# Order of the first six half products of a gated, quantized layer, and the way slot 2's weights are turned

## The chip, the cores and the metric

One core of one Trainium2 chip. The metric is device time of one execution in microseconds (us). A core has TensorE (PE, matrix products into PSUM banks), VectorE (DVE), ScalarE (ACT), GpSimd (POOL) and SyncE (SP), whose queue issues nearly all DMA transfers here. Each engine works through its own instructions strictly in the order in which the program lists them; engines wait for one another by semaphores.

## The reference

```python
# x: (4, 1024, 512), cond: (4, 128), norm_w: (512, 128), up_w: (4096, 512), down_w: (512, 2048)
scale = cond @ norm_w.T + 1.0
ms = jnp.mean(x * x, axis=-1, keepdims=True)
h = x * (scale[:, None, :] * jax.lax.rsqrt(ms + EPS))
u = h @ up_w.T
val, gate = jnp.split(u, 2, axis=-1)
h = val * jax.nn.gelu(gate, approximate=False)
hq = h + stop_gradient(act_quant(h) - h)              # 8 bit, one scale a token
wq = down_w + stop_gradient(weight_quant(down_w) - down_w)   # three values, one scale
y = hq @ wq.T
return y + x
```

## The kernel before

**Slots, halves, batches.** The 2048 hidden columns are cut into 16 slots of 128 (`NJ`); a slot needs 128 rows of the value weights and 128 of the gate weights of `up_w`. The 1024 tokens of a batch are cut into two halves of 512. "Half (j,h)" is slot j for half h of the first batch's tokens: a product for the gate (`pg`), Gelu on ScalarE, a product for the value (`pv`), then one VectorE instruction that scales and multiplies (L643, the "gate step"). `plain_half` (L635) does this; `plain_first` (L645) is half (0,0) with the work that brings in the data woven between its products. Each product is twelve matmuls of 128x128 by 128x512, because weights and tokens are each split into a high and a low half-precision part.

The first batch is computed by plain products. Batches 1 to 3 use a scheme with seven smaller products (L594, L668), for which seven combinations of each slot's weights are made once in the first batch, written to DRAM (`s_dram`) and loaded again for every batch.

**From a weight row to a product.** `w_load` (L284) loads a slot's weights by rows; `w_range` (L317) finds a power of two for each row (a reduction and three small instructions on VectorE); `w_gain` multiplies it with the token factor; `w_scale` (L328) scales the rows, on GpSimd for slots below `ROWS` and on ScalarE for the others. The weights must then be turned so that the contracted index lies on the partitions, in one of two ways:

- slots below `ROWS` (0, 1, 2): `w_turn` (L337), eight TensorE transposes into two PSUM banks; `w_high` (ScalarE) and `w_low` (VectorE) split the banks into high and low parts; `w_evac` (L381) copies the turned weights to `wf(j)` for the sums.
- the other slots: `w_rows` (L352) splits the rows (ScalarE copies, L357, VectorE subtracts, L358), then one turned DMA transfer on SP's queue (L359) of 512 KB.

`s_sums` (L385, GpSimd, four instructions, L391 to L394) forms the combinations in the buffer `sf`; `s_all` splits them (`s_high` on ScalarE, L403; `s_low` on GpSimd, L407) and writes them to DRAM (`s_spill`). For slots below `ROWS` the combinations are made of turned weights, so `s_load_x` and `s_load_y` (L431, L435) load them plainly (L429); for the others they are kept as rows and the load turns them (L427).

**Places.** `H` has 18 slots of buffer, which hold hidden results and, early on, other data. `X0 = H[:, 4:8]` holds the eight token tiles of the first batch (128 tokens each, tile n in half a slot). `W_SLOT`, `W_EARLY` and `ROW_SLOT` say which slot of `H` holds a slot's weight rows and their split.

**The start.** SP's queue first loads norm weights, token tiles 0 to 3, slot 0, slot 1, token tiles 4 to 7, slot 2 (L987 to L993). `first_sum` forms a tile's sum of squares (one instruction, 128x512, ScalarE or VectorE), `rsqrt` one small VectorE step and a power on GpSimd (L505), `first_scale` scales a tile, `first_turn` turns it by four TensorE transposes (L969), `first_high` and `first_low` split it (ScalarE L973, VectorE L977). `other_half` does the last three for tiles 4 to 7. `w_turn` of slots 1 and 2 takes place inside half (0,0) and half (1,0); `other_half` inside half (2,0).

The order of the halves is (0,0), (1,0), (2,0), (0,1), (1,1), (2,1), then (3,0), (3,1), (4,0) and so on. Between (2,0) and (0,1) VectorE's list has `cond_scale_rest` (L190) and `cond_largest`: the scale factors of batches 1 to 3 and their largest values, `mx`. `cond_over` (L209) turns `mx` on TensorE (`pm`), ahead of half (1,1). All of this is an order written out by hand (`manual_schedule`).

Of the kernel before, what the change touches and what calls it, by code (L numbers as in the profile page):

```python
# [51 lines left out]
def glu_quant_kernel(  # L52
# [17 lines left out]
    NK = D // P  # L70
# [103 lines left out]
    def cond_load_rest():  # L174
        v = cond[1:].rearrange("b c -> (b c)").partition_broadcast(P)
        ACT.dma_start(out=cb[:, 1:].rearrange("p b c -> p (b c)"), in_=v)
# [90 lines left out]
    sg0 = sm.tile([P, NJ, 2], F32, name="sg_0", tag="sg")  # L267
    up_v = up_w.rearrange("(t j p) d -> j p t d", t=2, p=P)
    W_SLOT = {1: 12, 2: 13, 0: 14}
    W_EARLY = {6: 9, 7: 10, 8: 11}  # L270
    ROW_SLOT = {3: 8, 4: 15, 5: 16}
    iv = {}
    pw = {}

    def wn(j):
        return H[:, W_EARLY.get(j, W_SLOT[j % 3])]

    def wf(j):

        return H[:, 11 if j == 2 else 15 + j % 2].rearrange("p t (n f) -> p (t n) f", n=2)  # L280

    sf = H[:, 17].rearrange("p t (n f) -> p (t n) f", n=2)

    def w_load(j, ts=(1, 0)):  # L284
        if j > 2:
            SP.dma_start(out=wn(j), in_=up_v[j])
            return
        for t in ts:
            SP.dma_start(out=wn(j)[:, t], in_=up_v[j][:, t])
# [27 lines left out]
    def w_range(j, t0=0, t1=2):  # L317
        w_factor(j, w_largest(j, t0, t1), t0, t1)

    def w_gain(j):  # L320
        DVE.tensor_tensor(sg0[:, j, :], sw[:, j, :], dx[:, 0:1].to_broadcast([P, 2]), ALU.mult)

    ROWS = 3
    LATE = 6

    def w_scale(j, ts=(1, 0), eng=None):  # L328
        eng = eng or (ACT if j >= ROWS else POOL)
        for t in ts:  # L330
            w, r = wn(j)[:, t], iv[j][:, t : t + 1]
            if eng is ACT:
                ACT.activation(w, w, AF.Copy, scale=r)
            else:
                eng.tensor_scalar(w, w, r, 1.0, ALU.mult, ALU.mult)

    def w_turn(j, banks=None, ts=(1, 0)):  # L337
        if j not in pw:
            pw[j] = banks or [po_bank(f"pw_{j}_{t}") for t in (1, 0)]
        for t in ts:  # L340
            n = 1 - t
            for k in range(NK):
                PE.transpose(  # L343
                    pw[j][n][:, k * P : (k + 1) * P], wn(j)[:, t, k * P : (k + 1) * P], ident
                )
# [6 lines left out]
    def w_rows(j):  # L352

        v = H[:, ROW_SLOT.get(j, 15 + j % 2)].bitcast(F16).rearrange("p t d -> p (t d)")
        n = v.rearrange("p (n w f) -> p n w f", n=4, w=2)
        f = wn(j).rearrange("p t (n f) -> p (t n) f", n=2)
        ACT.copy(n[:, :, 0], f)  # L357
        DVE.tensor_tensor(n[:, :, 1], f, n[:, :, 0], ALU.subtract)  # L358
        SP.dma_start_transpose(  # L359
            s_tile(j)[:, 3:7].rearrange("p n w (k f) -> p (n w k) f", k=2), v  # L360
        )

    def w_high(j, ts=(1, 0)):
        gate, a21, a22 = a_parts(j)
        g, v = (p.rearrange("p (n f) -> p n f", n=2) for p in pw[j])
        if 1 in ts:
            ACT.copy(gate[:, :, 0], g)
        if 0 in ts:
            ACT.copy(a21[:, 0], v[:, 0])
            ACT.copy(a22[:, 0], v[:, 1])  # L370

    def w_low(j, ts=(1, 0)):
        gate, a21, a22 = a_parts(j)
        g, v = (p.rearrange("p (n f) -> p n f", n=2) for p in pw[j])
        if 1 in ts:
            DVE.tensor_tensor(gate[:, :, 1], g, gate[:, :, 0], ALU.subtract)
        if 0 in ts:
            DVE.tensor_tensor(a21[:, 1], v[:, 0], a21[:, 0], ALU.subtract)
            DVE.tensor_tensor(a22[:, 1], v[:, 1], a22[:, 0], ALU.subtract)

    def w_evac(j):  # L381
        for n in range(2):
            ACT.copy(wf(j)[:, 2 * n : 2 * n + 2].rearrange("p n f -> p (n f)"), pw[j][n])

    def s_sums(j):  # L385
        if j >= ROWS:
            v = wn(j).rearrange("p t (n f) -> p t n f", n=2)
            a11, a12, a21, a22 = v[:, 1, 0], v[:, 1, 1], v[:, 0, 0], v[:, 0, 1]
        else:
            a11, a12, a21, a22 = (wf(j)[:, n] for n in range(4))  # L390
        POOL.tensor_tensor(sf[:, 0], a21, a22, ALU.add)  # L391
        POOL.tensor_tensor(sf[:, 2], a11, a21, ALU.subtract)
        POOL.tensor_tensor(sf[:, 1], sf[:, 0], a11, ALU.subtract)
        POOL.tensor_tensor(sf[:, 3], a12, sf[:, 1], ALU.subtract)  # L394
# [29 lines left out]
    def s_load(g, c0, c1, turn=False):  # L424
        s, d = s_tile(g)[:, c0:c1], s_dram[g % NJ, :, c0 * 2 * HALF : c1 * 2 * HALF]
        if turn:
            SP.dma_start_transpose(s.rearrange("p c w (k f) -> p (c w k) f", k=2), d)  # L427
        else:
            SP.dma_start(out=s.rearrange("p c w f -> p (c w f)"), in_=d)  # L429

    def s_load_x(g):  # L431
        s_load(g, Y_TO, C_ALL)
        s_load(g, 0, Y_FROM, g % NJ >= ROWS)

    def s_load_y(g):  # L435
        if g % NJ < ROWS:
            s_load(g, Y_FROM, Y_TO)
        else:
            s_load(g, Y_FROM + 1, Y_TO)
            s_load(g, Y_FROM, Y_FROM + 1, True)  # L440


    wmean = cpool.tile([P, 1], F32, name="wmean")
# [59 lines left out]
    def rsqrt(ssq, rs, eng=POOL):  # L503
        eng.tensor_scalar(ssq, ssq, 1.0 / D, EPS, ALU.mult, ALU.add)  # L504
        POOL.tensor_tensor(rs, ssq, neghalf[:, : rs.shape[-1]], ALU.pow)  # L505
# [129 lines left out]
    def plain_half(j, h, between=nothing):  # L635
        pg = bank(*(("A", 2) if h or j == 1 else ("B", 1)), name=f"pg_{j}_{h}")
        plain(j, 1, h, pg)
        t1 = wpool.tile([P, TOK], F32, name=f"g_{j}_{h}", tag="t1")
        ACT.activation(t1, pg, AF.Gelu, scale=gain(j, 1))
        between()  # L640
        pv = bank("E", 2, name=f"pv_{j}_{h}")
        plain(j, 0, h, pv)
        DVE.scalar_tensor_tensor(h_half(j, h), pv, gain(j, 0), t1, ALU.mult, ALU.mult)  # L643
# [279 lines left out]
    def first_load(n, m=1):  # L923
        SP.dma_start(
            out=X0[:, n : n + m],
            in_=xf[n * P : (n + m) * P, :].rearrange("(s p) d -> p s d", p=P),
        )
# [4 lines left out]
    def first_sum(n, eng=ACT):  # L932
        v, j, a = X0[:, n], junk[:, n % 4], ssq0[:, n : n + 1]
        if eng is ACT:
            ACT.activation(j, v, AF.Square, accum_out=a)
        else:
            eng.scalar_tensor_tensor(j, v, 1.0, v, ALU.mult, ALU.mult, accum_out=a)
# [21 lines left out]
    def first_scale(n, eng):  # L959
        r = rs0[:, n : n + 1]  # L960
        if eng is ACT:
            ACT.activation(X0[:, n], X0[:, n], AF.Copy, scale=r)
        else:
            eng.tensor_scalar(X0[:, n], X0[:, n], r, 1.0, ALU.mult, ALU.mult)
# [6 lines left out]
    def first_high(h, k, pt):  # L971
        c = slice(h * TOK, (h + 1) * TOK)
        ACT.activation(XP[:, 0, k, c], pt, AF.Copy, scale=scT[:, k, 0:1])  # L973

    def first_low(h, k, pt, eng=DVE):
        c = slice(h * TOK, (h + 1) * TOK)
        eng.scalar_tensor_tensor(  # L977
            XP[:, 1, k, c], pt, scT[:, k, 0:1], XP[:, 0, k, c], ALU.mult, ALU.subtract
        )
# [7 lines left out]
    first_load(0, 2)  # L987
    first_load(2, 2)
    w_load(0)
    w_load(1)  # L990
    first_load(4, 2)
    first_load(6, 2)
    w_load(2)  # L993
    keep_warm(3)
    pc = cond_first_row()
# [32 lines left out]
    w_range(0, 0, 1)  # L1028
    first_high(0, 0, ptx[0])
    w_high(0, (1,))  # L1030
    w_low(0, (1,))
    w_scale(0, (0,))
    w_gain(0)
    first_high(0, 1, ptx[1])
    first_high(0, 2, ptx[2])
    first_high(0, 3, ptx[3])
    cond_load_rest()
    w_range(1)
    w_gain(1)
# [3 lines left out]
    def second_part():  # L1043
        w_turn(0, ts=(0,))
        w_high(0, (0,))
        w_low(0, (0,))
        w_scale(1, (1,), ACT)
        for k in range(1, NK):
            first_low(0, k, ptx[k])
        ACT.activation(start_t, neghalf[:, 0:1], AF.Gelu)  # L1050


# [92 lines left out]
    def second_slot():  # L1145
        w_turn(1)
        w_high(1)
        w_low(1, (1,))
        w_range(2)
        w_gain(2)  # L1150
        w_scale(2)
        w_low(1, (0,))

    def third_slot():
        w_turn(2)
        w_high(2)
        w_low(2)
        w_evac(2)
        first_scale(4, ACT)
        first_scale(5, DVE)  # L1160
        first_scale(6, ACT)
        first_scale(7, DVE)

    def other_half():
        ptx = [po_bank(f"ptx_1_{k}") for k in range(3)] + [bank("A", 2, name="ptx_1_3")]
# [7 lines left out]
    w_load(3)  # L1173
    for n in range(4, ND):
        d_load(n)
    w_evac(0)
    w_evac(1)
    first_sum(4)
    first_sum(5)
    first_sum(6, DVE)  # L1180
    first_sum(7, DVE)
    rsqrt(ssq0[:, 4:8], rs0[:, 4:8], DVE)
    plain_half(1, 0, third_slot)
    w_load(4)
    s_sums(0)
    w_range(3)
    w_gain(3)
    plain_half(2, 0, other_half)
    w_load(5)
    for n in (2, 3):  # L1190
        d_load(n)
# [2 lines left out]
    s_sums(1)  # L1194
    cond_scale_rest()
    mx = cond_largest(1, B)
    plain_half(0, 1)
    w_range(4)
    w_gain(4)
    w_scale(4)  # L1200
# [3 lines left out]
    for n in D_SUM[0]:  # L1204
        d_sum(n)
    pm = cond_over(mx, 1, B, "po")
    plain_half(1, 1)
    w_load(6)
    for n in (0, 1):
        d_load(n)  # L1210
# [402 lines left out]
```

## Time and profile before

| What | Value |
|---|---|
| Runs | 728.81, 730.6, 730.28 us; median 730.28 |
| The profiled execution | 727.59 us, of it span 725.8 us |
| TensorE products, first 20 us | 17.23 us busy |
| TensorE products, 20 to 40 us | 19.78 us busy |
| TensorE products, 40 to 60 us | 19.69 us busy |
| TensorE products, 60 to 125 us | 65.0 us busy |
| TensorE clock granted | 1.00 throughout |
| Turned weight transfers (L359) | landing 4.3 to 6.7 us after issue, median 4.4 |
| Turned loads of combinations (L427) | 78 of them, issue median 1.39 us, landing 2.7 to 5.1, median 3.7 |
| Plain loads of combinations, 170 to 202 us (L429) | landing 2.7 to 4.2 us, median 3.4 |

A line of the profile names engine, source line, operation, tile, shape and count. In a timeline the first two numbers are start and duration in us; in square brackets stands how long the engine had been idle before, and what ended that. TensorE's matmuls are pipelined, so durations of neighbours overlap and the distances between starts tell what they cost.

### The profile page before, as it was taken

To read this page: it belongs to the slowest core of one execution; us is meant where nothing else is said; L and a number is where in the kernel's file an instruction comes from. 1 tells how busy PE (TensorE), PEld (TensorE's weight loads), DVE (VectorE), ACT (ScalarE), POOL (GpSimd) and SP (SyncE) were. 2 spreads that over 40 slices of the span, in tenths; PEclk is the share of its full clock that TensorE was granted. 3 is DMA by queue.
4 is the path that set the end of the run, shared out by engine and by line. 5 is a ranking of instruction groups with operands and counts; after the bars stand their busy time and mean duration, and the time that the engine had idled before them with its cause. 6 is when DMAs were issued, how large, how long until landed. Compare 5 with 4: busy or idle time off the path is not lost.

```text
span 725.8 us, 10153 instructions
## 1 busy us (share of the span) xinstructions
PE 719.1 (99%) x3664; PEld 359.2 (49%) x3664; DVE 581.7 (80%) x828; ACT 398.2 (55%) x627; POOL 193.5 (27%) x206
## 2 busy tenths in 40 slices
PE   8999999999999999999999999999999999999998
PEld 4544444444444446665444445665444444445844
DVE  8877888985698899787689897687678888755897
ACT  6869876772337674554335676544433665332374
POOL 1479897775100033440000030360020000000100
PEclk9999999999999999999999999999999999999999
DMA  7669998988354654876734646775934455442253
GB/s 265 224 188 299 291 287 237 263 190 227 117 103 102 131 156 129 203 170 164 181 98 101 131 102 179 195 158 162 219 102 102 86 118 101 88 115 89 98 180 116
DMA packets 203982, 117.30 MB, mean 162 GB/s; under 512 B 165382, under 2 KB 174487, under 8 KB 203932
## 3 DMA queue, kind: packets, MB, share of 16 engines
q1 hardware_dynamic: 203642, 116.33, 62.9%
q8 instruction: 28, 0.46, 0.3%
q10 hardware_dynamic: 290, 0.33, 0.1%
q14 instruction: 22, 0.18, 0.1%
HBM read 54.22 MB, written 23.09 MB: 107 GB/s over the span
## 4 chain that ended last, share of the span: by engine, by line
PE 95%; DVE 3%; DMA 1%; ACT 0%; issue 0%; SPq 0%; ACTq 0%
PE A L600 33%; PE E L600 17%; PE pg L615 11%; PE pv L615 10%; PE po L868 8%; PE B L600 8%; PE po_end L820 4%; PE po L820 1%; DMA H<-in_x_dram 1%; DMA SXY<-H 1%; DVE gm L734 1%; PE ptx L969 0%; PE pv L658 0%; DVE R L977 0%; PE pw L343 0%; PE po_B L868 0%
## 5 line engine op out<-in xcount | busy, mean ns | idle before, releaser
L600 PEld LDWEIGHTS <-SXY 128*128 128x128 f16 x2016 | 197.1, 98 | 232.4 <-issue 0.6
L600 PE MATMUL A<-R,SXY 128*128 128x512 f16 x1152 | 266.3, 379 | 0.0
L600 PE MATMUL E<-R,SXY 128*128 128x512 f16 x576 | 140.0, 379 | 0.1
L698 DVE SCALAR_TENSOR_TENSOR H<-A,sg,t 128x512 f32<-128x512 f32 x48 | 36.0, 750 | 69.8 <-PE A L600 69.7
L792 DVE TENSOR_TENSOR H<-H,am 128x1024 f32<-128x1024 f32 x64 | 76.2, 1217 | 0.0
L615 PEld LDWEIGHTS <-SXY 128*128 128x128 f16 x486 | 47.5, 98 | 57.5 <-DMA SXY<-H 0.8
L750 POOL PARTITION_ALL_REDUCE am<-R x8 | 14.3, 1793 | 228.9 <-DVE R L736 228.9
L711 ACT ACTIVATE t<-t,sg 128x512 f32<-128x512 f32 x48 | 34.6, 721 | 66.7 <-DVE t L708 66.5
L600 PE MATMUL B<-R,SXY 128*128 128x512 f16 x288 | 70.0, 379 | 0.0
L734 DVE TENSOR_REDUCE gm<-H 128x512 f32<-128x1024 f32 x56 | 69.0, 1232 | 1.0
L615 PE MATMUL pg<-R,SXY 128*128 128x512 f16 x252 | 57.8, 379 | 0.3 <-DMA SXY<-H 0.3
L615 PE MATMUL pv<-R,SXY 128*128 128x512 f16 x234 | 54.4, 380 | 0.0
L695 ACT ACTIVATE t<-B,sg 128x512 f32<-128x512 f32 x48 | 33.0, 687 | 36.2 <-PE B L600 36.2
L678 ACT COPY t<-A 128x512 f32<-128x512 f32 x48 | 27.9, 582 | 39.8 <-PE A L600 39.5
L504 POOL TENSOR_SCALAR ssq<-ssq 128x2 f32<-128x2 f32 x12 | 3.8, 320 | 172.1 <-ACT xt L534 122.8
L868 PE MATMUL po<-wd,R 128*128 128x256 fp8e4 x384 | 48.5, 273 | 0.0
L800 ACT ACTIVATE H<-H 128x1024 f32<-128x1024 f32 x38 | 39.9, 1050 | 14.3 <-DVE H L792 14.3
L690 ACT COPY v<-E 128x512 f32<-128x512 f32 x48 | 28.1, 585 | 30.8 <-PE E L600 27.5
L868 PEld LDWEIGHTS <-R 128*128 128x128 bf16 (+1 forms) x416 | 40.7, 98 | 8.6
L717 DVE SCALAR_TENSOR_TENSOR H<-v,sg,t 128x512 f32<-128x512 f32 x48 | 37.5, 782 | 7.9 <-ACT t L711 7.9
L736 DVE TENSOR_TENSOR R<-R,gm 128x512 f32<-128x512 f32 x56 | 41.6, 743 | 1.3
L714 DVE TENSOR_TENSOR v<-A,v 128x512 f32<-128x512 f32 x48 | 32.9, 685 | 12.1 <-PE A L600 11.0
(207 smaller groups left out, 982.3 us busy)
## 6 DMA issues: line engine op xcount, KB each, us to landing
SXY<-s_dram SPq DMA_DIRECT2D x57, 256.0 KB, 3.0
s_dram<-SXY SPq DMA_DIRECT2D x18, 384.0 KB, 3.0
H<-in_L_cond_up_w_dram SPq DMA_DIRECT2D x13, 512.0 KB, 5.2
SXY<-s_dram SPq DMA_DIRECT2D x39, 128.0 KB, 3.1
xr<-in_x_dram SPq DMA_DIRECT2D x19, 256.0 KB, 3.1
out_dram<-xr SPq DMA_DIRECT2D x19, 256.0 KB, 2.5
H<-in_x_dram SPq DMA_DIRECT2D x8, 512.0 KB, 8.3
R<-in_L_cond_down_w_dram SPq DMA_DIRECT2D x8, 512.0 KB, 6.1
```

Source lines behind the costliest of these rows:

```text
L600: PE.matmul(o, s[:, w, k, :], tv[:, :, c, l, k, :], start=start and n == 0, stop=stop and n == len(TERMS) - 1, skip_group_check=True,)
L615: PE.matmul(ps, a[k // 2][:, w, k % 2, :], XP[:, l, k, h * TOK : (h + 1) * TOK], start=n == 0, stop=n == len(terms) - 1,)
L695: ACT.activation(cur["t1"], pb, AF.Gelu, scale=gain(g, 1))
L698: DVE.scalar_tensor_tensor(h_half(g - 1, 0), prev["A"], gain(g - 1, 0), prev["t1"], ALU.mult, ALU.mult)
L711: ACT.activation(prev["t2"], prev["t2"], AF.Gelu, scale=gain(g - 1, 1))
L717: DVE.scalar_tensor_tensor(h_half(g - 1, 1), prev["v"], gain(g - 1, 0), prev["t2"], ALU.mult, ALU.mult)
L734: DVE.tensor_reduce(gm[0], v, AX.X, ALU.max, apply_absolute_value=True)
L736: return [largest, lambda: DVE.tensor_tensor(m, m, gm[0], ALU.max)]
L792: DVE.tensor_tensor(v, v, r.to_broadcast([P, 2, TOK]), ALU.mult)
L800: ACT.activation(v, v, AF.Copy, bias=MAGIC)
L820: PE.matmul(po.rearrange("p (y c o) -> p y c o", c=2, o=P), q[:, a, h, j], wd8[:, :, j // n, j % n, :, y0:y1].rearrange("p c o y -> p y c o"),
L868: PE.matmul(po, w[:, j], m, start=start and j == 0, stop=stop and j == n - 1, skip_group_check=True,)
```

## The change

The order of the halves becomes (0,0), (1,0), (0,1), (1,1), (2,0), (2,1). `ROWS` goes from 3 to 2, so slot 2 takes the way of the later slots: scaled by ScalarE, split as rows, turned by a DMA transfer (its rows in `H` slot 16). `w_evac` and `wf` are gone: the combinations of slots 0, 1 and 2 are formed from the rows, too, and all loads of combinations turn them. Slots 3, 4 and 5 get weight places of their own (`H` slots 11, 6, 7; 6 and 7 hold token tiles 4 to 7 until they are turned). Token tiles 4 to 7 are loaded ahead of slot 1; their sums of squares move into half (0,0), `other_half` from half (2,0) into half (1,0), and slot 1's second scaling from ScalarE to GpSimd. `w_range`, `w_gain`, `w_scale` and `w_rows` of slot 2 stand between halves (1,0) and (0,1).

```diff
-    W_EARLY = {6: 9, 7: 10, 8: 11}
-    ROW_SLOT = {3: 8, 4: 15, 5: 16}
+    W_EARLY = {3: 11, 4: 6, 5: 7, 6: 9, 7: 10, 8: 11}
+    ROW_SLOT = {2: 16, 3: 8, 4: 15, 5: 16}
...
-    ROWS = 3
+    ROWS = 2
...
-    def w_evac(j):
-        for n in range(2):
-            ACT.copy(wf(j)[:, 2 * n : 2 * n + 2].rearrange("p n f -> p (n f)"), pw[j][n])
...
     def s_sums(j):
-        if j >= ROWS:
-            v = wn(j).rearrange("p t (n f) -> p t n f", n=2)
-            a11, a12, a21, a22 = v[:, 1, 0], v[:, 1, 1], v[:, 0, 0], v[:, 0, 1]
-        else:
-            a11, a12, a21, a22 = (wf(j)[:, n] for n in range(4))
+        v = wn(j).rearrange("p t (n f) -> p t n f", n=2)
+        a11, a12, a21, a22 = v[:, 1, 0], v[:, 1, 1], v[:, 0, 0], v[:, 0, 1]
...
     def s_load_x(g):
         s_load(g, Y_TO, C_ALL)
-        s_load(g, 0, Y_FROM, g % NJ >= ROWS)
+        s_load(g, 0, Y_FROM, True)
 
     def s_load_y(g):
-        if g % NJ < ROWS:
-            s_load(g, Y_FROM, Y_TO)
-        else:
-            s_load(g, Y_FROM + 1, Y_TO)
-            s_load(g, Y_FROM, Y_FROM + 1, True)
+        s_load(g, Y_FROM + 1, Y_TO)
+        s_load(g, Y_FROM, Y_FROM + 1, True)
...
     w_load(0)
-    w_load(1)
     first_load(4, 2)
     first_load(6, 2)
+    w_load(1)
     w_load(2)
...
     w_high(0, (1,))
+    w_scale(0, (0,))
+    first_sum(4, DVE)
     w_low(0, (1,))
-    w_scale(0, (0,))
     w_gain(0)
     first_high(0, 1, ptx[1])
     first_high(0, 2, ptx[2])
     first_high(0, 3, ptx[3])
+    first_sum(5)
...
         w_high(0, (0,))
         w_low(0, (0,))
-        w_scale(1, (1,), ACT)
-        for k in range(1, NK):
-            first_low(0, k, ptx[k])
+        w_scale(1, (1,))
+        first_sum(6)
+        first_sum(7)
+        first_low(0, 1, ptx[1])
+        first_low(0, 2, ptx[2])
+        rsqrt(ssq0[:, 4:8], rs0[:, 4:8], DVE)
+        first_low(0, 3, ptx[3])
...
     def second_slot():
         w_turn(1)
         w_high(1)
-        w_low(1, (1,))
-        w_range(2)
-        w_gain(2)
-        w_scale(2)
-        w_low(1, (0,))
-
-    def third_slot():
-        w_turn(2)
-        w_high(2)
-        w_low(2)
-        w_evac(2)
         first_scale(4, ACT)
         first_scale(5, DVE)
-        first_scale(6, ACT)
-        first_scale(7, DVE)
+        w_low(1)
...
-    w_evac(0)
-    w_evac(1)
-    first_sum(4)
-    first_sum(5)
-    first_sum(6, DVE)
-    first_sum(7, DVE)
-    rsqrt(ssq0[:, 4:8], rs0[:, 4:8], DVE)
-    plain_half(1, 0, third_slot)
+    first_scale(6, ACT)
+    first_scale(7, DVE)
+    plain_half(1, 0, other_half)
     w_load(4)
     s_sums(0)
+    w_range(2)
+    w_gain(2)
+    w_scale(2)
     w_range(3)
     w_gain(3)
-    plain_half(2, 0, other_half)
+    w_rows(2)
+    plain_half(0, 1)
     w_load(5)
...
     cond_scale_rest()
     mx = cond_largest(1, B)
-    plain_half(0, 1)
+    plain_half(1, 1)
...
     pm = cond_over(mx, 1, B, "po")
-    plain_half(1, 1)
+    plain_half(2, 0)
```

More of the change, by code (lines that the diff above doesn't have):

```diff
@@ L276, in wn @@
         return H[:, W_EARLY.get(j, W_SLOT[j % 3])]
-    def wf(j):
-        return H[:, 11 if j == 2 else 15 + j % 2].rearrange("p t (n f) -> p (t n) f", n=2)
     sf = H[:, 17].rearrange("p t (n f) -> p (t n) f", n=2)
```

## The prediction

> **What bounds the kernel now.** I read the page first: engine totals, then TensorE's share by slice.
>
> ```profile
> span 725.8 us, 10153 instructions
> PE 719.1 (99%) x3664; PEld 359.2 (49%) x3664; DVE 581.7 (80%) x828; ACT 398.2 (55%) x627; POOL 193.5 (27%) x206
> PE   8999999999999999999999999999999999999998
> ```
>
> TensorE is busy for 99% of the span and only the first and last slice fall below 9. Its own pause list (who waited for whom, TensorE alone) shows what it ever waits for (the two lines left out are 0.4 and 0.2 us, ahead of 14 us):
>
> ```profile
> PE pz L985 <- DVE eps L915: 1.5, 1, 1.5
> PE pg L658 <- ACT SXY L367: 0.7, 1, 0.7
> ...
> PE pg L615 <- DMA SXY<-H: 0.3, 1, 0.3
> PE pm L211 <- DVE mx L204: 0.2, 1, 0.2
> ```
>
> All of it lies in the first 50 us. So the change can win only TensorE instructions that it removes plus these few waits, and can lose whatever new wait it puts there. The stretch that matters is from the end of half (0,0) at 19.68 us to the start of the fifth half at 38.34 us; TensorE's timeline there:
>
> ```profile
> 22.27 1.04 PE L343 MATMUL pw<-ident,H 128*128 128x128 f32 x8
> 23.15 0.60 PE L615 MATMUL pv<-R 128*128 128x512 f16 x2
> ...
> 28.33 1.91 PE L969 MATMUL ptx<-ident,H 128*128 128x128 f32 x16
> 30.07 2.75 PE L615 MATMUL pv<-R 128*128 128x512 f16 x12
> ...
> 38.23 0.27 PE L211 MATMUL pm<-ident,mx 128*3 128x128 f32 x1 [0.22 <-DVE mx L204]
> 38.34 2.75 PE L615 MATMUL pg<-R,SXY 128*128 128x512 f16 x12
> ```
>
> Starts are what counts (the ends overlap): twelve products take 2.59 us, a half 5.18; the eight turns of slot 2's weights 23.15 - 22.27 = 0.88; the sixteen turns of the second half's tokens 30.07 - 28.33 = 1.74. Work between 19.68 and 38.34 is 3 x 5.18 + 0.88 + 1.74 = 18.16 of 18.66 us, so about 0.50 us is the `pm` transpose and its wait. The chain of waits says who sets that: VectorE, not TensorE.
>
> ```profile
> 30.67 2.73 DVE R L977 x4
> 33.39 0.66 DVE H L643
> 34.05 1.68 DVE H L197
> ```
>
> **Removed: slot 2's turns on TensorE.** Eight transposes, -0.88 us, with TensorE busy on both sides. The high/low splits and the evacuations of slots 0 to 2 (ScalarE L383, about 0.58 each, six of them) go too; ScalarE and VectorE had idle time there, so they give nothing by themselves.
>
> **Moved: loads and half (0,0).** Slot 1's weights now follow all eight token tiles in SP's queue. Token loads 4-5 and 6-7 are issued at 4.31 and 5.1 us and take 8.3 us, so the last landed at 13.4; slot 1's second half takes that place and byte count, hence also 13.4. Slot 1's range starts at 13.27 now, so it is 0.15 late, and the extra VectorE square sum of tile 4 (0.69) fits the 0.70 us for which VectorE waits at 12.60. From there: reciprocal ready at 15.23 (15.08 now), GpSimd scales both halves of slot 1 by 16.7 (2 x 0.69), before its turns (17.08 now). Slot 0's second low parts end at 16.27 and 16.60; TensorE wants them at 16.22 and 16.65, so it slips about 0.1. The small rsqrt step (0.17 + gap) sits ahead of the last low part of the tokens, which ends near 18.77 against a need of 18.72: another 0.1. I take **+0.20** for half (0,0), between 0 (data earlier) and +1.2, if another 256 KB came ahead of them, 1.0 us at the first slice's 265 GB/s. On ScalarE three square sums (0.63 each) move ahead of the Gelu table load; the first fits the 0.61 idle at 14.92, the other two replace the 0.73 scale that GpSimd takes, so slot 1's high part starts 0.55 later, 18.27, against a need of 19.88.
>
> Half (1,0) then starts at 19.88. Its low weights are needed after four products, 0.87 later, at 20.75. VectorE first scales tile 5, once GpSimd's power (1.06) has ended near 19.1: 0.49 alone (9.77 us), 0.82 beside GpSimd (25.67 us); I take 0.82, because the sums of slot 0 run then. The low part follows, 0.69 (18.35 us), done at about 20.6: no wait, slack 0.1. Were GpSimd idle it would be 0.4. The Trainium skill ("SBUF — State Buffer", Who interferes with whom) says more: a `tensor_scalar` in a two-port mode and GpSimd exclude each other for a whole instruction. Behind one whole sum (0.72) the scale would end at 20.3, the low part at 21.0, and 0.2 to 0.3 us would be added to the sum; the row of 0.82 shows only 0.33 of blocking.
>
> The token turns stay, now inside half (1,0). Tiles 6 and 7 are scaled by 22.7, turned from 22.5 on in order 4 to 7: no wait. So half (1,0) ends at P = 19.88 + 5.18 + 1.74 = 26.80.
>
> **Added: the chain for slot 2 on VectorE.** Slot 3's present chain gives the lengths, from ScalarE's, VectorE's and SP's timelines:
>
> ```profile
> 42.40 1.03 ACT L357 CAST H<-H 128x1024 f16<-128x1024 f32 x1
> ...
> 43.46 1.23 DVE L358 TENSOR_TENSOR H<-H 128x1024 f16<-128x1024 f32 x1 [2.28 <-ACT H L357]
> ...
> 44.76 1.90 SPq L359 DMA_TRANSPOSE SXY<-H  x1
> ```
>
> After P, as after half (2,0) now (next group 32.66, gate 33.31), VectorE is free 0.65 later; gate step 0.66; range of slot 2 up to its reciprocal 1.80 (27.91 to 29.71); ScalarE scales and copies, VectorE subtracts 2.33 after the reciprocal (41.13 to 43.46); range of slot 3 fits in that gap; subtract 1.13 to the next start. So the gate of half (0,1) starts at P + 0.65 + 0.66 + 1.80 + 2.33 + 1.13 = P + 6.57, although its products were done at P + 5.18. Behind it in VectorE's order stand the condition sums (L197 to L204), for which `pm` waits, and behind `pm` on TensorE the whole of half (2,0). From gate to that half takes 38.34 - 33.31 = 5.03: start at P + 11.60 = 38.40. TensorE would be there at P + 10.36. The gap, 1.24, replaces 0.50: **+0.74**.
>
> The transfer itself: issue 3.63 after the reciprocal (41.13 to 44.76), P + 6.74 = 33.54; landing 4.37 later (the chain's `DMA SXY<-H`), 37.91, ahead of 38.40 by 0.49. Rows of that line go from 4.3 to 6.7, the tokens' turned transfers to 7.7. I take 4.37: that row, like this one, has an empty queue ahead. The bounds: 0 and 6.7 + 33.54 - 38.40 = +1.84. The Trainium skill differs with itself here: "Advanced Engine Details and Errata" (X-Bar Transpose (TRN2)) has turned transfers as fast as regular ones, "DMA: Bandwidth & Descriptors" (Latency and other measured facts) 261 GB/s where the middle dimension is not contiguous, an estimated 2.0 us for these 512 KB against 1.3 to 1.5. By either the data would be there before VectorE, and the sum would not move.
>
> SP's queue is in order: the loads of slot 5 and of two parts of the down weights now stand behind this transfer and go out near 35.5 instead of 23. Their readers come after 48 us; 1.5 MB at the first slice's 265 GB/s is 5.7 us. No cost; without that slack they would delay slot 3's transfer at about 45 us.
>
> **After 38.40** the order on all engines equals the present one from 38.34, with half (2,0) in the place of (1,1). VectorE sets both slot 3's transfer and the start, so the 0.31 wait at 49.17 stays. Slot 2's spill in three pieces adds two SP issues of about 0.5 with slot 5's transfer due more than 5 us ahead of its use.
>
> **Moved: loads of slots 0 to 2 in batches 1 to 3.** Nine slots, two turned transfers each instead of plain ones. Issue 1.39 and 1.19 against about 0.5; landing 3.7 (at most 5.1) against 3.4. They go out about one slot of 9.07 us ahead; issue plus landing is at most 6.5 of that. 39 slots already load so, and no TensorE wait falls there. Cost 0; without any lead, the excess of the part needed first, 9 x (0.89 + 0.3) = +10.7.
>
> **Sum:** +0.20 - 0.88 + 0.74 = +0.06. The profiled execution took 727.59 (span 725.8 and 1.8 around it), so 727.65; the median of the runs is 2.69 above it, 730.28 + 0.06, put up to the next tenth: **730.4 us**.
>
> **Rivals.** A difference under 0.3% (2.2 us) can't be told from none here.
> - *The gain is kept.* If the condition sums are ready in time, the transfer decides, 37.91 + 0.05: 0.38 less than now; if it too is early, -0.88 - 0.39 + 0.20 = -1.07. 729.2 to 729.9. For it: all the work is there, only its order is against it. Against: VectorE's order is fixed, and ScalarE's copy stands in between.
> - *Slot 2's weights come late* (the other side). Its packets share the engines with the 1.5 MB issued right behind: a landing 6.7 after issue, the longest row of its line, gives 40.2, 1.8 after VectorE is ready, of which slot 3's 0.31 is won back: 731.9. All 1.5 MB ahead of it, 5.3 us at the 299 GB/s of the fourth slice, gives 43.2 and 734.9. Priced between them, 733.4. It decides from a landing time of 4.9 us on. For: one row of 6.7 in a busy stretch. Against: the 44.76 transfer was also followed by loads, 3 us on.
> - *The turned loads miss their slot*: up to +10.7, 741.1. Against: 39 slots show no wait.
> - *It doesn't do what it says*: TensorE no longer turns slot 2, but stops as long for a number that has nothing to do with slot 2. That is my forecast.
>
> **Chances.** Forecast (729.9 to 731.2) 0.57; gain kept 0.17; late transfer 0.18, half of it past 732.5; missed slots 0.08. Faster by over 0.3% has no mechanism, only scatter of runs (728.81 to 730.6): 0.07. Slower: 0.09 + 0.08 + 0.04 scatter = 0.21. Same 0.72. The range runs from 728.6, below the kept gain, to 733.4, the late transfer's price.
>
> **What would show it.** TensorE's wait for `pm` of about 1 us instead of 0.2 and half (2,0) near 38.4; turned transfer out near 33.5 and landed by 38; no third set of weight turns; half (1,0) starting near 19.9; no TensorE wait after 55 us. A TensorE wait on a transfer into `R` before half (2,0), a first half ending after 20.5, or waits at the batches' starts would make it wrong.

## The result, and the profile after

| Kernel | Median, us | Lowest to highest | Runs |
|---|---|---|---|
| before | 728.75 | 728.12 to 730.82 | 14 |
| after | 730.44 | 729.39 to 732.19 | 14 |

The ratio of after to before is 1.0018, 95% interval 1.001 to 1.0027: 0.7 to 2.0 us slower, under the 2.2 us named in the prediction as what can't be told from no change, but a loss all the same. The forecast of 730.4 us was made from an early median of 730.28 for the kernel before; with more runs that median came down by 1.5 us and the change cost about 1.7, so the two errors cancel: that the time came out so near is luck. The difference, not the time, has to be explained: +0.06 was forecast.

The page of the kernel after (its span, engine totals, TensorE by slice):

```profile
span 729.3 us, 10132 instructions
PE 720.3 (99%) x3656; PEld 359.0 (49%) x3656; DVE 582.6 (80%) x824; ACT 396.4 (54%) x622; POOL 193.2 (26%) x205
PE   8989999999999999999999999999999999999998
```

TensorE has eight instructions less (x3656 against x3664), the turns of slot 2's weights. A new 8 stands in the third slice, 36 to 55 us. TensorE's own waits say what it is (engine, tile, line, what it waited for, total, times, longest):

```profile
PE pg L601 <- DMA SXY<-H: 1.8, 1, 1.8
...
PE pm L211 <- DVE mx L204: 1.0, 1, 1.0
```

Both existed before, at 0.3 and 0.2. TensorE's timeline, in which line 601 is the plain product (615 before):

```profile
7.89 3.77 PE L971 MATMUL pz<-H 128*128 128x512 f16 x9
11.50 1.91 PE L955 MATMUL ptx<-ident,H 128*128 128x128 f32 x16
...
21.58 2.87 PE L601 MATMUL pg<-R,SXY 128*128 128x512 f16 x12
24.29 1.91 PE L955 MATMUL ptx<-ident,H 128*128 128x128 f32 x16
...
40.19 0.27 PE L211 MATMUL pm<-ident,mx 128*3 128x128 f32 x1 [1.04 <-DVE mx L204]
40.52 2.76 PE L601 MATMUL pg<-R 128*128 128x512 f16 x12
...
52.85 2.76 PE L601 MATMUL pg<-R,SXY 128*128 128x512 f16 x12 [1.79 <-DMA SXY<-H]
```

Half (1,0) starts at 21.58, half (2,0) at 40.52, half (3,0) at 52.85. The profiled execution is 3.5 us longer than that of before (729.3 against 725.8), in three stretches:

| Stretch | before | after | difference |
|---|---|---|---|
| start to half (1,0) | 19.68 | 21.58 | +1.90 |
| half (1,0) to half (3,0) | 29.49 | 31.27 | +1.78 |
| half (3,0) to the end | 676.63 | 676.45 | -0.18 |

The first is the nine warming matmuls (`pz`): 3.61 us from their start to the token turns here, 1.96 in the first profile of before, the rest 0.25 ahead of them. From the first product (14.52 here, 12.62 before) to half (1,0) it is 7.06 in both. This belongs to the execution and not to the change: two experiments whose code is that of after up to the end of half (0,0), loads first and both cures, took 2.37 and 2.29 us there, with a short wait for ScalarE in it, and their first product stands at 13.42 and 13.31, against 13.63 in a second profile of before. Both and more, the same up to there, was slow (3.64). The other two stretches sum to +1.60, near the difference of the medians, 1.69. That it is so near is partly chance: the second profile of before is 0.68 longer behind half (3,0), and against it the sum is +0.91. The middle stretch is the steady part, 29.49 and 29.50 in the two profiles of before, 31.27 and 31.44 in the two of after.

In the middle stretch the chain of waits has two transfers that now set TensorE's start:

```profile
35.47 5.01 DMA R<-H
40.47 0.05 issue
40.52 2.76 PE pg L601 x12
...
48.48 4.32 DMA SXY<-H
52.80 0.05 issue
52.85 2.76 PE pg L601 x12
```

The first is slot 2's turned transfer, landed at 40.47; the second slot 3's. That one left SP only at 48.48, although its data were ready two microseconds earlier, at 46.53, by VectorE's subtract:

```profile
45.30 1.23 DVE L354 TENSOR_TENSOR H<-H 128x1024 f16<-128x1024 f32 x1 [2.28 <-ACT H L353]
```

SP's timeline and its waits show why; line 355 is the turned transfer of weights, 282 the weight load, 444 the load of down weights, 400 the spill:

```profile
35.47 2.12 SPq L355 DMA_TRANSPOSE R<-H  x1
37.70 0.84 SPq L282 DMA_DIRECT2D H<-in_L_cond_up_w_dram  x1
38.59 0.95 SPq L444 DMA_DIRECT2D R<-in_L_cond_down_w_dram  x2
39.92 0.35 SPq L400 DMA_DIRECT2D s_dram<-SXY  x1
48.48 1.77 SPq L355 DMA_TRANSPOSE SXY<-H  x1
```

```profile
SPq L355 <- DMA s_dram<-SXY: 8.1, 1, 8.1
```

Slot 3's weights go into the buffer from which slot 0's combinations are spilled, so the transfer waits for the spill to land. SP's timeline of the kernel before, and its wait for the same spill between 34 and 52 us (lines 411, 359 and 458 are now 400, 355 and 444):

```profile
23.86 0.88 SPq L458 DMA_DIRECT2D R<-in_L_cond_down_w_dram  x2
37.87 0.35 SPq L411 DMA_DIRECT2D s_dram<-SXY  x1
44.76 1.90 SPq L359 DMA_TRANSPOSE SXY<-H  x1
```

```profile
SPq L359 <- DMA s_dram<-SXY: 3.2, 1, 3.2
```

So the kernel before had this wait, too; there it ended ahead of the data (43.46 to 44.69 for the subtract) and cost nothing. The spill's time from issue to landing, after (L400, issued at 39.92) and before (L411, issued at 37.87):

```profile
DMA to landing us min/median/max: 8.5/8.5/8.5
...
DMA to landing us min/median/max: 3.6/3.6/3.6
```

Just ahead of it now stand three loads of 512 KB (slot 5, two parts of the down weights), which formerly went out before 25 us.

### The profile page after: what moved, and what is told of

Read it like the earlier page. It is cut to its first block, busy times and chain, and to the rows that moved or that the text cites. A ratio compares the mean times of both kernels' runs of the same rounds, so it can differ in the third digit from the quotient of the medians.

```text
span 729.3 us, 10132 instructions
## 1 busy us (share of the span) xinstructions
PE 720.3 (99%) x3656; PEld 359.0 (49%) x3656; DVE 582.6 (80%) x824; ACT 396.4 (54%) x622; POOL 193.2 (26%) x205
## 4 chain that ended last, share of the span: by engine, by line
PE 96%; DMA 2%; DVE 1%; ACT 1%; issue 0%; SPq 0%; ACTq 0%
PE A L586 34%; PE E L586 17%; PE pg L601 10%; PE pv L601 10%; PE B L586 9%; PE po L854 8%; PE po_end L806 4%; PE po L806 1%; DMA R<-H 1%; DMA H<-in_x_dram 1%; DMA SXY<-H 1%; PE pz L971 1%; PE ptx L955 0%; PE pv L644 0%; PE po_B L854 0%
```

## The experiments

All kernels compute the same layer. "Stretch" is the time from half (1,0) to half (3,0) in the run's profile.

| Kernel | Median, us | Ratio to before | 95% interval | Stretch, us |
|---|---|---|---|---|
| before | 728.75 | | | 29.49 |
| before again | 729.31 (one run) | | | 29.50 |
| after | 730.44 | 1.0018 | 1.001 to 1.0027 | 31.27 |
| after again | 730.46 | 1.0024 | 1.0013 to 1.0034 | 31.44 |
| loads first | 728.19 | 0.9997 | 0.9987 to 1.0006 | 29.35 |
| pm behind | 730.44 | 1.0027 | 1.0017 to 1.0037 | 31.10 |
| range first | 728.99 | 1.0004 | 0.9994 to 1.0014 | 29.16 |
| rows as sums alone | 730.06 | 1.0007 | 0.9994 to 1.0019 | 29.53 |
| both cures | 728.47 | 0.9988 | 0.9979 to 0.9998 | 28.52 |
| both and more | 728.20 | 0.9981 | 0.9968 to 0.9994 | 27.86 |

Medians of before in the two later sets were 728.72 and 729.06; the ratios are to these.

**After again.** Unchanged.

> The changed kernel once more, for a second profile. Theory S (start clock): its first profile stands 1.90 us behind the kernel before already at the token turns (11.50 against 9.60 us), because nine warming matmuls ran at 0.42 us each instead of 0.22; that belongs to the execution and not to the change, so in this profile the nine may take 2.1 us again, and from the token turns on everything keeps its distances: TensorE waits of about 1.0 us for pm and 1.5 to 1.8 us for slot 3's transfer. Rival: the shift belongs to the new order of loads, and the nine take 3.8 us again. Ratio to the kernel before 1.001 to 1.003 by both.

The nine matmuls were slow again, 3.90 us. TensorE's waits were 1.0 us for `pm` and 1.9 at half (3,0); this profile puts the latter down to ScalarE (L448), but SP's wait for the spill is there as before, 8.3 us, and the spill took 8.7 to land. So this profile alone does not decide between the start clock and the load order; loads first and both cures, with the same load order up to there and 2.12 us, do. Ratio as expected.

**Loads first.** Slot 5's load and the two parts of the down weights go out ahead of slot 2's transfer.

```diff
     w_load(4)
+    w_load(5)
+    for n in (2, 3):
+        d_load(n)
     s_sums(0)
...
     plain_half(0, 1)
-    w_load(5)
-    for n in (2, 3):
-        d_load(n)
```

> The loads of slot 5 and of two parts of the down weights go out right behind slot 4's load, ahead of slot 2's turned transfer. Theory Q (queue): in the changed kernel slot 0's spill landed 8.5 us after its issue because 1.5 MB of loads went out just ahead of it, and slot 3's turned transfer waited for that spill. Then here the spill lands about 3.6 us after issue, TensorE's wait for slot 3 falls from 1.8 to 0.3 us, slot 2's transfer lands in 4.4 instead of 5.0 us, and the time is 1.5 to 1.8 us below the changed kernel, about that of the kernel before. Rival: spill and transfers are slow by themselves in this stretch, and the time stays that of the changed kernel.

Its SP timeline:

```profile
34.36 1.94 SPq L355 DMA_TRANSPOSE R<-H  x1
38.82 0.36 SPq L400 DMA_DIRECT2D s_dram<-SXY  x1
45.50 1.71 SPq L355 DMA_TRANSPOSE SXY<-H  x1
```

The spill lands 3.6 us after issue, slot 3's transfer leaves as soon as VectorE has finished its data, and TensorE's list has no wait for it. The stretch falls by 1.9 us and the median by 2.3; the ratio's interval holds 1. That is the queue theory's answer, a little more than it asked (1.5 to 1.8 us). The wait for `pm` is still 1.0 us. One part of the expectation failed: slot 2's transfer landed 5.0 us after its issue as before (34.36 to 39.37 in the chain of waits), not 4.4, although no load stood behind it any more.

**pm behind.** The transpose of the condition maxima moves behind half (2,0) on TensorE.

```diff
-    pm = cond_over(mx, 1, B, "po")
     plain_half(2, 0)
+    pm = cond_over(mx, 1, B, "po")
```

> The turn of the condition maxima (pm) is moved behind half (2,0) on TensorE. Theory T: in the changed kernel slot 2's transfer landed at 40.47, just before half (2,0) began at 40.52, so without pm half (2,0) still begins when the transfer lands; TensorE's wait of 1.0 us for pm becomes one of about 1.4 us for the transfer, and the time changes by less than 0.3 us. Rival V: VectorE's condition sums are all that holds half (2,0); it then begins 1.2 us earlier and the time falls by 1.2 us.

TensorE's waits:

```profile
PE pg L601 <- DMA SXY<-H: 1.5, 1, 1.5
PE pz L971 <- DVE eps L901: 1.5, 1, 1.5
PE pg L601 <- DMA R<-H: 1.4, 1, 1.4
```

The wait for VectorE is gone and one of 1.4 us for slot 2's transfer stands in its place; the time is unchanged. In the kernel after, VectorE and the transfer end 0.2 us apart: taking away VectorE's part gives nothing, and taking away the transfer's alone, which no run does, could give no more than these 0.2.

**Range first.** Slot 2's range moves in VectorE's list to where that engine stands idle for 2.4 us.

```diff
+    w_range(2)
+    w_gain(2)
     plain_half(1, 0, other_half)
...
     s_sums(0)
-    w_range(2)
-    w_gain(2)
```

> The range of slot 2 is put ahead of half (1,0) in VectorE's list, where VectorE stands idle for 2.4 us; everything else stays. Theory: slot 2's transfer goes out 3.6 us earlier, the condition sums end 1.2 us earlier, the wait for pm falls from 1.0 to 0.2 us, and the three loads behind the transfer go out 3.6 us earlier too, so that slot 0's spill lands before slot 3's transfer wants to go: TensorE's wait for slot 3 about 0.3 us. Time 2.5 us below the changed kernel, 0.8 to 1.2 below the kernel before. Rival (slot 3's wait has another cause than the queue): only 1.0 to 1.2 us below the changed kernel.

TensorE's waits in the stretch:

```profile
PE pm L211 <- DVE mx L204: 0.5, 1, 0.5
...
PE pg L601 <- DMA SXY<-H: 0.5, 1, 0.5
```

Both waits shrink to 0.5, neither to the 0.2 and 0.3 expected; the median falls by 1.5, between the two expectations. Slot 2's transfer left 2.5 us earlier (11.37 us after the start of half (1,0) instead of 13.89), not 3.6, because ScalarE scales slot 2 only after the token splits. The three loads moved with it, but so did the spill (38.42), which still took 7.9 us and still held slot 3's transfer:

```profile
SPq L355 <- DMA s_dram<-SXY: 7.5, 1, 7.5
```

VectorE's condition product (L197) took 2.64 us instead of 1.75, having begun while GpSimd was already at its low parts; that ate part of the gain.

**Before again**, for a second profile, and **rows as sums alone**: the kernel before with `wf` and `w_evac` no longer used, sums from the rows, the weight places of the change and all combinations loaded turned.

> The kernel before once more, for a second profile. Theory S (start clock): whether the nine warming matmuls take 2.1 or 3.7 to 3.9 us belongs to the execution, so it may be either here; from the token turns to half (3,0) it is 39.6 us in any case (39.57 in the first profile). Rival: the kernel before always starts at 2.1.

> The kernel before with one part of the change alone: sums of slots 0 to 2 kept as rows, all loads of combinations turned, no evacuations; half order, loads at the start and slot 2's turns on TensorE stay (slot 4's and 5's loads go behind the token turns, since their places hold tokens). My theory: turned loads are hidden, ratio to the kernel before 0.999 to 1.001, no TensorE wait after 60 us. Rival (turned loads cost at the batches' starts): 1.002 or more with such waits.

```diff
-    W_EARLY = {6: 9, 7: 10, 8: 11}
+    W_EARLY = {3: 11, 4: 6, 5: 7, 6: 9, 7: 10, 8: 11}
...
-        s_load(g, 0, Y_FROM, g % NJ >= ROWS)
+        s_load(g, 0, Y_FROM, True)
...
-    w_evac(0)
-    w_evac(1)
...
     plain_half(2, 0, other_half)
+    w_load(4)
     w_load(5)
```

The second profile of before has the stretch unchanged (29.50) and its nine matmuls took 2.76 us to the token turns, part of that a wait for ScalarE. From the token turns to half (3,0) it is 39.82 us, not 39.6: behind that wait the turns took 1.98 us to what follows them instead of 1.74. With sums from rows alone the stretch is 29.53, TensorE waits for nothing after 60 us, and the interval holds 1. Turned loads cost nothing that the trace shows; the time leaves room for up to 1.4 us (1.0019), and no wait in which it could lie.

**Both cures.** Loads first and range first together.

> The changed kernel with both cures: loads ahead of slot 2's transfer, and slot 2's range ahead of half (1,0). From the token turns to half (3,0) 39.1 us (41.35 in the changed kernel, 39.67 and 39.44 with one cure each), because the first cure leaves the pm wait of 1.0 and the second left 0.5 for slot 3. Time 0.3 to 0.8 us below either single cure, ratio to the kernel before 0.998 to 1.000. Rival (the two cures remove the same wait): equal to the better single one.

```profile
38.42 0.27 PE L211 MATMUL pm<-ident,mx 128*3 128x128 f32 x1 [0.49 <-DVE mx L204]
```

That is the only TensorE wait in the stretch. From the token turns to half (3,0) it is 38.84 us, against 39.1 expected; the ratio is in the range forecast. The median, 728.47, is not below that of loads first (728.19, another set), so the gain over a single cure is shown by the stretch (0.8 and 0.6 us) and only indicated by the times.

**Both and more.** In addition `pm` behind half (2,0), and slot 3's split and transfer ahead of slot 4's range:

```diff
     plain_half(1, 1)
+    w_rows(3)
     w_range(4)
     w_gain(4)
     w_scale(4)
-    w_rows(3)
```

> As with both cures, and pm behind half (2,0), and slot 3's split and transfer ahead of slot 4's range and scaling on VectorE and ScalarE. Theory: no TensorE wait is left between the token turns and half (3,0), which then takes 38.1 to 38.4 us; time 0.7 to 1.0 us below both cures alone, ratio to the kernel before 0.996 to 0.999: the full gain of the removed turns. Rival: a later slot's transfer is late in its turn (slot 4, whose split moves back 1.2 us on VectorE), and half of the gain is given back there.

```profile
39.06 2.75 PE L601 MATMUL pg<-R 128*128 128x512 f16 x12
41.66 2.75 PE L601 MATMUL pv<-R 128*128 128x512 f16 x12
44.24 0.27 PE L211 MATMUL pm<-ident,mx 128*3 128x128 f32 x1
44.35 2.75 PE L601 MATMUL pg<-R 128*128 128x512 f16 x12
46.94 2.75 PE L601 MATMUL pv<-R 128*128 128x512 f16 x12
49.53 2.75 PE L601 MATMUL pg<-R,SXY 128*128 128x512 f16 x12
```

No bracket is left: halves follow at 5.18 us, `pm` costs 0.11. From the token turns to half (3,0) it is 37.95 us, a little less than expected, and no later slot waits. Of the 0.7 to 1.0 us expected below both cures, the stretch shows 0.66 and the medians 0.27. This version beats both kernels: ratio to before 0.9981, interval 0.9968 to 0.9994. Of the 1.63 us off the stretch (29.49 to 27.86), 0.88 are the removed turns and 0.87 the two gaps that the kernel before had (0.39 at `pm`, 0.48 ahead of half (3,0)), less the 0.12 below. Whether a new order alone would have won the 0.87 in the kernel before, no run shows.

## Why the prediction was near in time and wrong in its sum

- **Removed turns, -0.88: as stated.** TensorE has eight instructions less, and in both and more, without waits, nothing takes their place.
- **Half (0,0), +0.20: nothing.** First product to half (1,0) is 7.06 us with either order, in the profiles that started early too (loads first: 13.42 to 20.48). Slot 1's weights were in time. (A first half that ended after 20.5 us was named as a sign of being wrong; it ended at 21.58, but in the second profile of before at 20.69, so this sign can't tell the change from the start.)
- **Slot 1's low weights, "no wait, slack 0.1": +0.12.** The first twelve products took 2.71 (21.58 to 24.29) instead of 2.59. Scaling tile 5 beside GpSimd took 0.96 us, not the 0.82 taken, and half (1,0) came 0.20 sooner than the sum had it. The Trainium skill's rule ("SBUF — State Buffer", Who interferes with whom) warned of this at the right place. The measured block, 0.96 - 0.49 = 0.47, is less than the 0.73 of GpSimd's sum beside it (20.89 to 21.62), for all of which the rule would block; GpSimd's spans are rough, so this does not settle it.
- **The chain for slot 2 on VectorE, +0.74: right in mechanism, +1.03.** The chain ran as worked out, here by VectorE's timeline (range, gate step, first condition sum):

```profile
29.93 1.22 DVE L290 TENSOR_REDUCE wam<-H 128x2 f32<-128x1024 f32 x1
...
35.35 0.75 DVE L629 SCALAR_TENSOR_TENSOR H<-pv,sg,g 128x512 f32<-128x512 f32 x1
36.02 1.75 DVE L197 TENSOR_TENSOR H<-R 128x1536 f32<-128x1536 f32 x1
```

  Half (1,0) ended at P = 28.63; the gate step of half (0,1) began at P + 6.72 (forecast 6.57), `pm` at P + 11.56, and by VectorE alone half (2,0) would have begun 0.11 later, at 40.30. Slot 2's transfer added 0.22, where the sum had it 0.49 ahead of VectorE: it left at P + 6.84 (forecast 6.74) but landed 5.0 us after issue, not 4.37. That row was slot 3's; why slot 2's took longer is open, and the loads behind it are not the reason (loads first). The gap is 40.52 - 38.99 = 1.53 against 0.50.
- **SP's queue, "No cost": this step failed, +1.48.** The prediction named the three loads that the transfer holds back, looked for the readers of those loads, found them late enough, and stopped. What stood behind the loads in the same queue, slot 0's spill, was not asked for; slot 3's transfer waits for that spill, and the wait list of the kernel before had the line. It landed 8.5 us after issue instead of 3.6, and TensorE's wait, which the prediction kept at 0.31, rose to 1.79. Loads first takes exactly this away. (The 5.7 us for three loads of 512 KB at 265 GB/s should be 5.9; nothing rests on it.)
- **After half (3,0), 0: right as far as the profiles can tell.** -0.18 here, but this stretch runs from 676.4 to 677.3 over all ten profiles, 676.63 and 677.31 in the two of before. TensorE has no wait after 60 us; the turned loads are hidden.

The sum as measured, -0.88 + 0.12 + 1.03 + 1.48 = +1.75, is the 1.78 of the stretch. The rival "slot 2's weights come late" had the right kind of cause, a transfer made late by 1.5 MB of loads, on the wrong transfer: the loads went out behind slot 2's and ahead of the spill. Slot 2's own transfer did decide the start of half (2,0), as that rival's condition (a landing from 4.9 us on) asks, but by 0.22 us and without help from the loads.

## What to carry to other kernels

When a waiting transfer holds back others in an ordered queue, follow each held transfer to what is queued behind it, not only to its own readers: a transfer that has to land before a buffer is free counts like a reader, too. When two chains end within a few tenths of each other, taking one away shows little; the pair has to go. And a removed TensorE instruction is worth its time only after the engines that lose the cover have been given a new order: the same removal was +1.3 us (ratio 1.0018) in one order and -1.4 us (0.9981) in another, which also closed two gaps that the kernel before had.

## What the runs showed of the hardware

**The start.** Nine equal matmuls behind the first scale step took 2.12 us in some profiles and 3.65 to 3.90 in others: 2.12 in both profiles of before, in rows as sums alone, loads first and both cures; 3.77 to 3.90 in both profiles of after, pm behind and both and more. Range first shows a change and its reversal:

```profile
3.63 2.08 PE L971 MATMUL pz<-H 128*128 128x512 f16 x5
...
8.06 0.35 PE L236 MATMUL pd<-dg,one 1*128 1x1 f32 x2 [1.60 <-DVE newton L939]
8.34 3.65 PE L971 MATMUL pz<-H 128*128 128x512 f16 x9
```

The same five matmuls take 2.31 us in every other profile. In range first the profile's rows give a granted clock of 0.50 from 8.75 to 12.17 us, 3.4 us long, and 1.00 around it. In the other profiles they give 1.00 from the start, even where a matmul took 0.42 us, so there the slow clock is inferred from the matmuls alone. The Trainium skill ("TensorE: Matmul & The Clock Gate", Part 1: The HAM clock gate (the "warmup" mystery)) describes a gate that halves the clock until a window of about 3.4 us has been busy, a window that does not start with the kernel. The rows agree: 3.4 us at half the clock in range first, 0.42 us a matmul or 0.22 in the others, with the changeover at different places in kernels whose first 6 us are alike. From their start to the token turns the slow nine take 3.5 to 3.7 us and the fast ones 1.96 where nothing else holds TensorE; the first product starts at 14.52 to 15.00 us in the slow profiles and at 12.62 to 13.63 in the others. That is about as much as the change. Whether the order of loads shifts the odds is not settled by ten profiles; that the medians follow the stretch (the cures lower both) speaks against it.

**Turned transfers of 512 KB** into the same place landed 5.0 us after issue in after, after again and pm behind, and 4.4 in range first, with the same loads behind them each time, and 5.0 in loads first with none behind it. So the loads behind are not the cause; what is stays open. All are above the 1.3 to 2.0 us that the prediction estimated from bandwidths.
